# The last 256 rows of a gated cross-attention: the norm's weights multiplied in on GpSimd beside the squares, and one factor per row behind the root

## The chip, the cores and the metric

The kernel runs on one core of a Trainium2 chip. The metric is device time in microseconds (us) of one execution. The core has five engines that run their own queues of instructions and wait for each other through semaphores: TensorE (PE, matmuls; PEld its weight loads), VectorE (DVE), ScalarE (ACT), GpSimd (POOL) and SyncE (SP), which here issues nearly all transfers.

## The reference

Everything is float32. x has 8 batches of 1024 rows of 1024; the memory has 8 batches of 64 rows of 512. Cut to what is computed:

```
memory_proj = memory @ W_mem.T                          # 8 x 64 x 1024
scores      = x @ memory_proj.T / sqrt(1024)
attn        = softmax(scores)
context     = attn @ memory_proj                        # 8 x 1024 x 1024
gate        = sigmoid(concat(x, context) @ W_gate.T + b_gate)
fused       = x + gate * context
out         = fused * rsqrt(mean(fused**2) + 1e-6) * norm_w
```

The mean goes over the 1024 elements of a row. norm_w has one weight for each column.

## The kernel before

The kernel first projects the memory, and folds the context's part of the gate into a second projection of the memory, so that the only large product is x with the first half of W_gate. It works on 16 blocks (q = 0 to 15) of 512 rows each, a block being four tiles (t = 0 to 3) of 128 rows. The large product of a block uses a two-level scheme with fewer multiplications than the plain one: seven outer products, emitted in the order 1, 6, 7, 5, 4, 2, 3 (`ORDER`, L599), each of seven inner products (named A to F, A twice) in `outer_product` (L753). The inner sums of inputs (tiles `l`) and the sums `gate<-gate,u` run on GpSimd; the sums that read matmul results run on VectorE, all through the helper `tt` (L95). So L95 stands for many additions, and its rows are told apart by the names of their tiles.

The order of the work is written out by hand. Every inner product advances a counter `slot`; `at(slot, f, ...)` puts a function on a list that is emitted when the counter gets there (`step`, L646), and a loop at the end (L900) empties what is left. All instructions are kept in the order in which they are emitted on each engine, and each engine runs its queue in that order. The framework adds the waits between engines from the tiles that each instruction reads and writes.

In a block, outer products 5 and 4 complete the gate of tiles 2 and 3 (one half of 512 columns each), and 2 and 3 that of tiles 0 and 1: half 0 with outer product 2, half 1 with outer product 3. For each half, ScalarE takes the sigmoid (L657) and VectorE multiplies by the context, which lies in the accumulation buffer `pc` (L653). In blocks 0 to 14 x is added by a transfer, and the norm follows inside the next block's work.

The last block (q = 15) has functions of its own. x is loaded into a tile `xl` early (`load_last`, L702). `last_gated` (L709) multiplies by the context, adds x on VectorE (L714, in the profile `gate<-gate,xl`) and takes the sum of squares of the half on ScalarE (L719), the first half's sum being brought into a bias (L722). `sqrt_table` (L748) loads ScalarE's table for the root ahead of the squares of the last half. `last_root` (L727) takes the root per row, `last_norm` (L736) has VectorE take the reciprocal (L740, with half 0 alone), multiply a half by that number per row and by norm_w's columns in one instruction with two tensor inputs (L744), and has SyncE issue the store of the half (L98, 256 KB).

For tiles 3 and 2 this is placed among the inner products of the outer products 2 and 3 (L871, the case o == 4); so some L744 of tile 2 stand in VectorE's queue among the last sums. For tiles 1 and 0 (d = 1 goes ahead of c = 0) it comes after the last matmul. In VectorE's queue the end is: L744 of tile 2's second half, the sums with kE and kF, product with pc and addition of x for tile 1, the same for tile 0, then L740 and two L744 for tile 1, L740 and two L744 for tile 0. GpSimd's queue ends with three additions `gate<-gate,u` of outer product 3. ScalarE's ends with two sigmoids, the table load, and square and root of tile 1, then of tile 0.

Of the kernel before, what the change touches and what calls it, by code (L numbers as in the profile page):

```python
# [9 lines left out]
AF = mybir.ActivationFunctionType  # L10
ALU = mybir.AluOpType
# [4 lines left out]
P = 128  # L16
# [4 lines left out]
def tile_gated_cross_attention_rmsnorm(  # L21
# [42 lines left out]
    nc = tc.nc  # L64
# [4 lines left out]
    NQ = B * QPB  # L69
# [3 lines left out]
    H = 512  # L73
# [15 lines left out]
    pin = tc.keep_in_program_order  # L89
# [4 lines left out]
    def tt(eng, o, a, b, op):  # L94
        pin(eng.tensor_tensor(o, a, b, op))  # L95

    def load(o, i):
        pin(nc.sync.dma_start(o, i))  # L98

    def t4k(pool, shape, tag, name):  # L100
        return pool.tile(shape, F32, tag=tag, name=name)
# [33 lines left out]
    for k in range(KD):  # L135
        t = t4k(*((gpool, [P, D], "gate") if k < 7 else (apool, [P, D], "s4")), f"w2_{k}")
# [8 lines left out]
    nw_sb = const.tile([P, D], F32, name="nw_sb")  # L145
# [184 lines left out]
    A, S, L2, O = {}, {}, {}, {}  # L330
    sTs, attns, attnTs, scs, mps, mgs = {}, {}, {}, {}, {}, {}
    def where(q, t=0):
        return q // QPB, (q % QPB) * QT + t * P
# [258 lines left out]
    def at(slot, fn, *args):  # L592
        due.setdefault(slot, []).append(lambda: fn(*args))

    def mid(key, fn, *args):
        beside.setdefault(key, []).append(lambda: fn(*args))
# [47 lines left out]
    slot = 0  # L644
# [55 lines left out]
    xl, halves = {}, {}  # L700
# [35 lines left out]
    def last_norm(t, h):  # L736
# [8 lines left out]
        )  # L745
        load(out[b, n0 : n0 + P, cols], g)

    def sqrt_table():  # L748

        t = t4k(small, [P, 1], "warm", "warm")  # L750
        pin(nc.scalar.activation(t, eps_sb, AF.Sqrt))

    def outer_product(q, o, ext):  # L753
# [68 lines left out]
        if ext:  # L822
            row, h, g = ext
# [3 lines left out]
            for r, names in ((0, ("A", "F")), (1, ("E", "D"))):  # L827
                pc = ps_ctx.tile([P, H], F32, tag="ctx", name=f"pc{q}_{o}_{r}")
                for n in range(2):
                    cols = slice(h * H + n * C, h * H + (n + 1) * C)  # L830
# [36 lines left out]
        if o in (4, 3) and q + 1 == NQ:  # L867
            c, d = 2 * ext[0], 2 * ext[0] + 1
            if o == 3:
                sqrt_table()  # L870
            when = (4, 5, 7, 9, 11, 12) if o == 4 else (2, 4, 5, 6, 7, 8)  # L871
            at(slot + when[0], last_root, d)
            at(slot + when[1], last_root, c)
            for w_, (t, h_) in zip(when[2:], ((d, 0), (d, 1), (c, 0), (c, 1))):
                at(slot + w_, last_norm, t, h_)
        elif o in (4, 3):

            row = ext[0]
            c, d = 2 * row, 2 * row + 1
            for t in (d, c):  # L880
                at(slot + 5, residual, q, t)
            if row == 0:
                when = (17, 18, 23, 29, None, None)
            else:
                when = (17, 18, 23, 25, 29, 32)
            at(slot + when[0], square, q, c)
            at(slot + when[1], square, q, d)
            for w_, (t, h_) in zip(when[2:], ((c, 0), (c, 1), (d, 0), (d, 1))):
                if w_ is None:
                    mid((q + 1, 4), norm, q, t, h_)  # L890
                else:
                    at(slot + w_, norm, q, t, h_)
# [3 lines left out]
    for q in range(NQ):  # L896
        plan(q)
        for o, ext in ORDER:
            outer_product(q, o, ext)
    while due:  # L900
        slot = min(due)
# [27 lines left out]
```

## Time and profile before

| what | value |
|---|---|
| device time, median of 3 runs | 972.3 us (972.01 to 973.57) |
| the profiled execution's own time | 972.48 us |
| its span, first to last instruction | 970.7 us |
| busy: TensorE, VectorE, ScalarE, GpSimd | 958.1, 815.0, 329.2, 763.5 us |
| last matmul starts, length of the group of four | 959.69 us, 1.03 us |
| last GpSimd instruction | ends 959.49 us |
| second of the last two sigmoids ends | 961.91 us |
| table load for the root | 961.93 to 963.21 us |
| roots of tiles 1 and 0 end | 964.36 and 965.30 us |
| last four L744 | 964.59 to 966.01 and 966.12 to 967.54 us |
| last four stores issued | 965.37, 966.04, 966.90, 967.56 us |
| from issue to landing of such a store | 2.0 to 2.1 us |

Times inside the execution count from the start of the span. A row of the timeline has start, length, engine, line, operation, the tile written and the tiles read, the sizes and how many were merged; in brackets the idle time before it and who ended it. A row of a group has its count, busy time, mean length in ns and idle time ahead of it. "SPq" or "POOLq" is the engine's own queue of issuing and waiting instructions, which is not counted as busy.

### The profile page before, as it was taken

What the parts mean: (1) busy time and instruction counts of PE and PEld (TensorE: products, weight loads), DVE (VectorE), ACT (ScalarE), POOL (GpSimd) and SP (SyncE); (2) the same over time, 40 slices, a digit from 0 to 9 for tenths busy, and PEclk for the clock granted to TensorE, in tenths of its full rate; (3) what the DMA queues carried; (4) which work ended last, traced back from release to release, by engine and by line L of the source; (5) the groups of instructions that cost most, each with busy time, mean ns of one, the idle gap of its engine ahead of it and who ended that gap; (6) DMA issues with size and microseconds to landing.
All of it is one profiled execution on the core that took longest, in us unless ns stands there. A gap on an engine that the chain in (4) does not pass through costs nothing.

```text
span 970.7 us, 14400 instructions
## 1 busy us (share of the span) xinstructions
PE 958.1 (99%) x4986; PEld 773.3 (80%) x4986; DVE 815.0 (84%) x1483; ACT 329.2 (34%) x603; POOL 763.5 (79%) x889
## 2 busy tenths in 40 slices
PE   9999999999999999999999999999999999999995
PEld 8546878788888888788888888888888878888884
DVE  5988879879797988879797988979797978979787
ACT  2000234161423334162433324152333325152345
POOL 4998878778786968878786978878687878878692
PEclk9999999999999999999999999999999999999998
DMA  9957573472919374482918374381918465391712
GB/s 374 280 137 166 95 134 95 118 165 73 177 65 169 107 134 102 109 175 65 185 65 159 102 140 111 96 187 57 193 66 148 113 131 119 87 196 48 190 67 86
DMA packets 71159, 128.32 MB, mean 132 GB/s; under 512 B 12336, under 2 KB 49200, under 8 KB 70832
## 3 DMA queue, kind: packets, MB, share of 16 engines
q1 hardware_dynamic: 61760, 93.34, 36.7%
q0 software_dynamic: 9184, 33.56, 19.0%
q8 instruction: 39, 0.64, 0.3%
q10 hardware_dynamic: 144, 0.52, 0.2%
q14 instruction: 32, 0.26, 0.1%
HBM read 87.56 MB, written 41.68 MB: 133 GB/s over the span
## 4 chain that ended last, share of the span: by engine, by line
PE 97%; DVE 1%; DMA 1%; issue 0%; ACT 0%; DVEq 0%
PE kA L92 20%; PE pc L92 12%; PE kE L92 11%; PE kD L92 10%; PE kF L92 10%; PE kC L92 10%; PE kB L92 10%; PE psT L92 6%; PE pg L92 5%; PE pm L92 3%; DMA memq<-in_mem 1%; PE pa L438 0%; PE sc L412 0%; DVE gate L744 0%; DVE it L95 0%
## 5 line engine op out<-in xcount | busy, mean ns | idle before, releaser
L95 POOL TENSOR_TENSOR gate<-gate,u 128x256 f32<-128x256 f32 x336 | 287.5, 886 | 107.2 <-DVE u L95 107.2
L657 ACT ACTIVATE gate<-gate 128x512 f32<-128x512 f32 x128 | 80.6, 631 | 306.5 <-DVE gate L95 305.9
L95 POOL TENSOR_TENSOR l<-a 128x256 f32<-128x256 f32 x128 | 124.6, 974 | 21.6 <-PE kA L92 20.4
L344 DVE STREAM_TRANSPOSE a<-xq 128x512 f32<-128x512 f32 x128 | 137.9, 1099 | 2.9 <-DMA mgd<-mpq 2.9
L92 PE MATMUL pc<-mg,attnT 64*128 64x256 f32 x512 | 127.5, 389 | 0.0
L92 PE MATMUL kB<-it,l 128*128 128x256 f32 x448 | 115.1, 379 | 0.4 <-DVE gate L95 0.4
L92 PE MATMUL kD<-it,l 128*128 128x256 f32 x448 | 115.0, 379 | 0.0
L92 PEld LDWEIGHTS pc<-mg,attnT 64*128 64x128 f32 x512 | 90.6, 186 | 29.9 <-issue 21.2
L686 DVE SCALAR_TENSOR_TENSOR gate<-gate,ss,nw_sb 128x512 f32<-128x512 f32 x120 | 109.0, 918 | 1.1
L95 POOL TENSOR_TENSOR l<-s 128x256 f32<-128x256 f32 x96 | 79.3, 826 | 33.1 <-PE kF L92 30.3
L92 PE MATMUL kA<-w,a 128*128 128x256 f32 x384 | 98.6, 379 | 0.0
L92 PEld LDWEIGHTS kB<-it,l 128*128 128x128 f32 x448 | 85.0, 190 | 12.3 <-DVE gate L95 0.8
L92 PEld LDWEIGHTS kD<-it,l 128*128 128x128 f32 x448 | 85.1, 190 | 11.6
L95 DVE TENSOR_TENSOR gate<-gate,pc 128x512 f32<-128x512 f32 x128 | 86.8, 679 | 0.4 <-ACT gate L657 0.4
L95 DVE TENSOR_TENSOR gate<-gate,kE 128x256 f32<-128x256 f32 x112 | 45.5, 418 | 48.4 <-PE kE L92 42.3
L92 PEld LDWEIGHTS kA<-w,a 128*128 128x128 f32 x384 | 71.7, 190 | 9.5 <-DVE mg_c L95 0.2
L810 ACT COPY u<-kA 128x256 f32<-128x256 f32 x112 | 40.5, 361 | 110.5 <-PE kA L92 106.1
L92 PE MATMUL kE<-it,a 128*128 128x256 f32 x256 | 69.0, 392 | 0.0
L671 ACT ACTIVATE junk<-gate 128x1024 f32<-128x1024 f32 x60 | 63.5, 1059 | 11.2 <-DMA gate<-in_x 10.2
L95 DVE TENSOR_TENSOR u<-u,kB 128x256 f32<-128x256 f32 x112 | 45.7, 408 | 24.2 <-PE kB L92 21.6
L92 PE MATMUL kA<-t,s 128*128 128x256 f32 x256 | 65.8, 379 | 0.0
L92 PE MATMUL kF<-w,l 128*128 128x256 f32 x256 | 65.7, 379 | 0.0
(141 smaller groups left out, 2055.6 us busy)
## 6 DMA issues: line engine op xcount, KB each, us to landing
xq<-in_x SPq DMA_DIRECT2D x64, 512.0 KB, 10.1
gate<-in_x POOLq DMA_DIRECT2D x60, 512.0 KB, 8.1
out<-gate SPq DMA_DIRECT2D x60, 512.0 KB, 2.6
w<-in_w_gate_t SPq DMA_DIRECT2D x8, 512.0 KB, 11.0
w<-in_w_gate_t SPq DMA_DIRECT2D x2, 2048.0 KB, 16.2
mg<-mgd SPq DMA_DIRECT2D x16, 256.0 KB, 3.8
mpd<-mpT SPq DMA_DIRECT2D x4, 512.0 KB, 7.7
mgd<-mpq SPq DMA_DIRECT2D x16, 128.0 KB, 3.4
```

Source lines behind the costliest of these rows:

```text
L92: pin(nc.tensor.matmul(o, lhsT, rhs, start=start, stop=stop, skip_group_check=True))
L95: pin(eng.tensor_tensor(o, a, b, op))
L344: nc.vector.transpose(A[key][:, :, r * P : (r + 1) * P], chunks(xq[q][:, 4 * t : 4 * t + 4, :], KD)[:, half * KH : (half + 1) * KH],)
L657: pin(nc.scalar.activation(g, g, AF.Sigmoid))
L671: nc.scalar.activation(junk, O[q, t], AF.Square, accum_out=ss[:, t % 2 : t % 2 + 1])
L686: nc.vector.scalar_tensor_tensor(g[:, cols], g[:, cols], rstd[:, t % 2 : t % 2 + 1], nw_sb[:, cols], ALU.mult, ALU.mult,)
L810: pin(nc.scalar.copy(p1, kb["A"]))
```

## The change

For tiles 1 and 0 of the last block alone, the multiplication by norm_w is taken out of the instruction behind the root. GpSimd multiplies x + gate * context by norm_w into the tile `xl`, which is free once x has been added: both half-0 pieces behind its last additions, the half-1 pieces each behind the addition of x. ScalarE goes on squaring the unweighted sum. Behind the root, VectorE takes the reciprocal and multiplies a half by the number per row (`tensor_scalar`, no second tensor); of the last tile, half 0 is multiplied on ScalarE (a copy with a scale per row). The stores read `xl`: tile 1 half 0, tile 1 half 1, tile 0 half 1, and at the end tile 0 half 0. Tiles 2 and 3 go on as before.

```diff
+    def weigh(t, h):
+
+        cols = slice(h * H, (h + 1) * H)
+        tt(nc.gpsimd, xl[t][:, cols], O[NQ - 1, t][:, cols], nw_sb[:, cols], ALU.mult)
+
+    def last_scale(t, h, on_act):
+        b, n0 = where(NQ - 1, t)
+        rstd = halves[t][0][:, 2:3]
+        cols = slice(h * H, (h + 1) * H)
+        g = xl[t][:, cols]
+        if on_act:
+            pin(nc.scalar.activation(g, g, AF.Copy, scale=rstd))
+        else:
+            pin(nc.vector.tensor_scalar(g, g, rstd, None, ALU.mult))
+        load(out[b, n0 : n0 + P, cols], g)
+
+    def last_reciprocal(t):
+        rstd = halves[t][0][:, 2:3]
+        pin(nc.vector.reciprocal(rstd, rstd))
...
-            when = (4, 5, 7, 9, 11, 12) if o == 4 else (2, 4, 5, 6, 7, 8)
-            at(slot + when[0], last_root, d)
-            at(slot + when[1], last_root, c)
-            for w_, (t, h_) in zip(when[2:], ((d, 0), (d, 1), (c, 0), (c, 1))):
-                at(slot + w_, last_norm, t, h_)
+            if o == 4:
+                at(slot + 4, last_root, d)
+                at(slot + 5, last_root, c)
+                for w_, (t, h_) in zip((7, 9, 11, 12), ((d, 0), (d, 1), (c, 0), (c, 1))):
+                    at(slot + w_, last_norm, t, h_)
+            else:
+                for t in (d, c):
+                    at(slot, weigh, t, 0)
+                for i, t in enumerate((d, c)):
+                    at(slot + 2 + i, weigh, t, 1)
+                    at(slot + 2 + i, last_root, t)
+                at(slot + 4, last_reciprocal, d)
+                at(slot + 4, last_scale, d, 0, False)
+                at(slot + 4, last_scale, d, 1, False)
+                at(slot + 4, last_reciprocal, c)
+                at(slot + 4, last_scale, c, 1, False)
+                at(slot + 4, last_scale, c, 0, True)
```

## The prediction, on record before the run

> **What bounds the kernel now.** First the page: engine shares and the chain that ended last.
>
> ```profile
> PE 958.1 (99%) x4986; PEld 773.3 (80%) x4986; DVE 815.0 (84%) x1483; ACT 329.2 (34%) x603; POOL 763.5 (79%) x889
> ...
> PE 97%; DVE 1%; DMA 1%; issue 0%; ACT 0%; DVEq 0%
> ```
>
> TensorE is the bound until its last matmul. The order of instructions shows that the change leaves TensorE's queue as it was and touches only the ends of the other queues. So the whole question is the tail after 960.7 us. The chain in order of time (start, length, what) shows that tail:
>
> ```profile
> 959.86 0.88 PE kF L92 x4
> ...
> 961.28 0.63 ACT gate L657
> ...
> 961.93 1.28 ACT L751
> ...
> 963.42 0.62 ACT junk L719 x2
> ...
> 964.59 1.42 DVE gate L744 x2
> ...
> 966.12 0.75 DVE gate L744
> ```
>
> After TensorE come the second sigmoid, the table load of the root, squares, root, and four L744 normalizations on VectorE, each followed by its store. The stores:
>
> ```profile
> out<-gate SPq DMA_DIRECT2D x4, 256.0 KB, 2.1
> ```
>
> They are issued at 965.37, 966.04, 966.90 and 967.56. The last lands 2.06 us after its issue, at 969.62; barriers end the span at 970.70. In the view of DMA, bytes flow from 966.2 to about 969.2, and two transfers fill one unbroken stretch of 1.40 us: 0.70 each. So the tail has two limits: last issue + 2.06, and first issue + 0.85 (to the first bytes) + 4 x 0.70 + 0.40 (last bytes to landing) = first issue + 4.05, if the four come close together.
>
> Next the timeline, VectorE against GpSimd, for what happens when both read at once:
>
> ```profile
> 156.52 1.29 DVE L686 SCALAR_TENSOR_TENSOR gate<-gate,ss,nw_sb 128x512 f32<-128x512 f32 x1
> ...
> 156.54 0.72 POOL L95 TENSOR_TENSOR l<-s,l 128x256 f32<-128x256 f32 x1
> ...
> 375.92 0.74 DVE L686 SCALAR_TENSOR_TENSOR gate<-gate,ss,nw_sb 128x512 f32<-128x512 f32 x1
> ...
> 375.98 1.27 POOL L95 TENSOR_TENSOR l<-s,l 128x256 f32<-128x256 f32 x1
> ...
> 937.66 0.72 POOL L95 TENSOR_TENSOR l<-a 128x256 f32<-128x256 f32 x1
> ...
> 937.74 1.19 DVE L95 TENSOR_TENSOR gate<-gate,xl 128x512 f32<-128x512 f32 x1
> ...
> 958.15 0.75 DVE L744 SCALAR_TENSOR_TENSOR gate<-gate,halves,nw_sb 128x512 f32<-128x512 f32 x1
> ...
> 958.26 1.23 POOL L95 TENSOR_TENSOR gate<-gate,u 128x256 f32<-128x256 f32 x1
> ...
> 959.48 0.75 DVE L744 SCALAR_TENSOR_TENSOR gate<-gate,halves,nw_sb 128x512 f32<-128x512 f32 x1
> ```
>
> Of two such instructions one runs in its usual time (VectorE 0.69 to 0.75, GpSimd 0.73) and the other waits for it. GpSimd wins when it starts first, and even 0.02 us later (156.54); VectorE wins when it starts about 0.06 or more ahead (375.92). A waiting VectorE instruction ends 0.55 after GpSimd's (938.93 against 938.38); a waiting GpSimd instruction of 256 elements ends 0.59 after VectorE's (959.49 against 958.90).
>
> **What the Trainium skill says.** "SBUF — State Buffer", section "Who interferes with whom": VectorE with two SBUF inputs, or in a two-port mode such as `tensor_scalar` may enter, shares a read and write port pair with a GpSimd instruction that reads SBUF; whoever is first keeps it for the whole instruction and the other blocks. The rows above agree for two inputs; no `tensor_scalar` on SBUF stands in this trace. "VectorE: DVE Perf Modes", section "The perf-mode tier table": float32 `tensor_scalar` on SBUF reaches 2x. With the same page's (N+151)/0.96 ns, which gives 0.69 for 512 elements as the additions of x measure, 256 cycles are 0.42 us: an estimate. "ScalarE: Activation LUTs", section "What ACT_TABLE_LOAD costs": 186 ns + 0.833 ns per element, and 93 more for a pointer operand. The squares (0.61) agree; a scaled copy is then 0.70, an estimate.
>
> **The change, part by part.** Tile 1 goes ahead of tile 0; each has halves 0 and 1.
>
> Removed: four L744 of 0.75 on VectorE. Added: three scalings there at 0.42, one on ScalarE at 0.70, and four 128x512 multiplications on GpSimd. For these the set-up shows 1.27 with nothing in the way:
>
> ```profile
> L95 POOL TENSOR_TENSOR it<-w,it 128x512 f32<-128x512 f32 x4 | 5.1, 1274 | 0.2
> ```
>
> I take 1.27; multiplying instead of subtracting could cost nothing or some tenths more. Were all covered, the first scaling would end at 964.59 + 0.42 and its store be issued at 965.04 instead of 965.37. But the first two multiplications start while VectorE still has sums of the last half to do, and the other two start right behind an addition of x, so all four lie among VectorE's two-input instructions. Followed in order of time:
>
> 1. GpSimd's last addition ends at 958.26 + 1.23 = 959.49. The multiplication for (1,0) is queued behind it, its inputs ready, and starts about 0.04 before that end, 959.45 (GpSimd's instructions overlap so, 943.96 against 944.00), until 960.72. VectorE's L744 of tile 2 at 959.48 comes 0.03 too late, and ends at 960.72 + 0.55 = 961.27 instead of 960.23: **+1.04**. Queued behind it on VectorE: the additions of kE and kF, for which both sigmoids wait.
> 2. The multiplication for (0,0) waits for that L744 and ends at 961.27 + 0.59 + 0.54 (256 more elements: 1.27 - 0.73) = 962.40.
> 3. kE's addition ends at 961.61, kF's at 961.94; the second sigmoid ends at 962.81 (was 961.91); the table load follows, and squares can start at 964.23 (was 963.33).
> 4. Product with the context for tile 1: 962.30 to 962.98. Addition of x: to 963.70 (was 962.67). Product for tile 0: to 964.30.
> 5. The multiplication for (1,1), released by the addition of x, starts 0.08 later (956.44 after 956.36 shows that delay): 963.78 to 965.05. The addition of x for tile 0, due at 964.34, waits and ends at 965.60 (was 963.99): **+1.61**.
> 6. The root of tile 1 is ready at 965.26, but its reciprocal is behind that addition on VectorE: 965.52 to 965.68. The multiplication for (0,1) starts at 965.68 and ends at 966.95. The scaling of (1,0), due at 965.72, comes 0.04 too late; if it runs in the two-port mode it ends at 966.95 + 0.28 (its 256 cycles after the release) = 967.23; L744 there ended at 965.34: **+1.89**.
> 7. The rest: scaling (1,1) to 967.57, reciprocal of tile 0 to 967.65, scaling (0,1) to 968.10, ScalarE's (0,0) to 968.38. Stores are issued at 967.26, 967.62, 968.13 and 968.51. SyncE's issue takes 0.33, so it keeps up.
> 8. First issue + 4.05 = 971.31; last issue + 2.06 = 970.57 is covered by it. Against 969.62: **+1.7**.
>
> The store of (0,0) is last in SyncE's queue and waits for ScalarE; nothing is behind it. ScalarE's copy stands at the end of its queue, so it needs no table load that would stop others. GpSimd's closing DRAIN ends at 962.56, 3.07 after its last addition; after 966.95 that is 970.02, under the last landing.
>
> The profiled execution took 972.48 for a span of 970.70, 0.18 over the median of 972.3. 972.3 + 1.7 = **974.0**. The shorter instructions save 3.00 - 1.26 on VectorE and the waiting takes back more: slower by 0.17%, inside what counts as no change below.
>
> **The rivals.**
> - **The scaling doesn't take GpSimd's ports** (step 6 alone fails: 1x mode, 0.69). The first scaling ends at 966.41, its store is issued at 966.44, landing 970.49: +0.9, 973.2. For: no such row in the trace. Against: the skill's two pages.
> - **L744 of tile 2 is first in step 1.** The margin is 0.09. Then (1,0) ends at 961.36, (0,0) at 962.59, the first addition of x at 963.14, (1,1) at 964.49, the second addition at 965.04, (0,1) at 966.39, the first scaling at 966.67: issue 966.70, landing 970.75, +1.1: 973.4. Against: the row at 156.54.
> - **On the other side: no collision holds VectorE.** Mechanism: GpSimd's multiplications let VectorE's two-input instructions go first or run beside them, so the roots stay at 964.36 and 965.30. First issue 965.04, landing 969.09: -0.5, 971.8. It decides if each GpSimd multiplication ends before VectorE's next two-input instruction, under about 0.7 us at step 1. Against: all rows above, and 1.27 for the nearest multiplication.
> - **Slower by over 0.2%: GpSimd multiplies slower than it subtracts.** Three of its four instructions lie on the path (steps 1, 5, 6), so each 0.1 us of price costs 0.3. From 1.36 us on, the loss is over 1.94 us; at 1.5 it is 2.4, 974.7.
>
> **How the numbers follow.** About 0.2%, 1.94 us, is what a measurement can tell from no change here. Chances: both blocks as followed, 974.0, 0.52; scaling unblocked, 973.2, 0.17; L744 first, 973.4, 0.10; dearer multiplication, 974.3 to 974.9, 0.13; no collision, 971.8, 0.08. The main case spreads by some 0.3 with the transfers (0.70 to 0.76 each) and the run; about a fifth of it lies over 974.24. Slower by over 0.2%: 0.11 + 0.12 = 0.23. Faster by over 0.2% is under 970.36, beyond even the case without collisions: 0.02. Within: 0.75. The range 973.0 to 974.7 takes in 973.2, 973.4, the main case with its spread and half of the dearer one.
>
> **What would show it.** Step 1: L744 of tile 2 at 959.48 takes about 1.8 instead of 0.75, with GpSimd's first 128x512 ending 0.55 before it. Step 5: the last addition of x takes about 1.26 instead of 0.69. Step 6: the first scaling takes about 1.5 and the next 0.42; 0.69 for both would mean 1x. Step 8: one stretch of DMA of 2.8 us after 968. The prediction is wrong if a row of 128x512 on GpSimd isn't 1.27 when nothing holds it, or if the last store's landing isn't what ends the span.

## The result, and the profile after

| | before | changed |
|---|---|---|
| median of 22 runs each | 972.65 us | 974.32 us |
| ratio, 95% interval | | 1.0018 (1.0012 to 1.0024) |
| span of the profiled execution | 970.7 us | 972.5 us |
| last matmul's end to the end of the span (trace) | 9.98 us | 11.70 us |
| last four stores issued | 965.37, 966.04, 966.90, 967.56 | 967.34, 967.77, 968.40, 968.83 |

The kernel became slower by 0.18%. A ratio of 1 lies outside the interval, so the loss is real. The interval reaches past 0.2%, so the times don't settle on which side of the prediction's bound of 0.2% the loss lies. The prediction was 974.0 against 972.3, a ratio of 1.0017. Both kernels were measured some 0.3 us above these two figures, so it is the difference that is to be compared: 1.67 us here, 1.7 predicted. Nearly all of it lies behind the last matmul: the tail is 1.72 of the 1.81 us by which the two profiled spans differ. In its profile, the changed kernel is already 0.09 us late at the last group of four matmuls (it starts at 959.79 instead of 959.69); 0.09 is to be taken off its times below before they are set beside those of before.

The chain that ended last, in order of time, in the changed kernel (start, length, what):

```profile
960.88 0.40 issue
961.28 0.42 DVE gate L95
...
961.72 0.64 ACT gate L657
...
963.10 1.30 DVE gate L95 x2
...
964.43 1.26 DVE gate L95
...
965.87 1.84 DVE xl L761 x2
...
967.87 0.72 ACT xl L759
```

In the kernel before, the chain went from the second sigmoid over the table load and the squares to four L744. Here the table load and the squares are no longer in it. VectorE's own queue takes their place: the row at 963.10 is the first addition of x with the product behind it, the one at 964.43 the second addition, and then come the scalings at L761. The first row is 0.40 us in which VectorE's queue shows no wait: it is held by an L744 that is still under way. The timeline of both engines says why:

```profile
959.54 1.26 POOL L95 TENSOR_TENSOR xl<-gate,nw_sb 128x512 f32<-128x512 f32 x1
...
959.58 1.78 DVE L744 SCALAR_TENSOR_TENSOR gate<-gate,halves,nw_sb 128x512 f32<-128x512 f32 x1
...
960.77 1.71 POOL L95 TENSOR_TENSOR xl<-gate,nw_sb 128x512 f32<-128x512 f32 x1
...
963.87 1.27 POOL L95 TENSOR_TENSOR xl<-gate,nw_sb 128x512 f32<-128x512 f32 x1 [1.39 <-DVE gate L95]
...
964.43 1.26 DVE L95 TENSOR_TENSOR gate<-gate,xl 128x512 f32<-128x512 f32 x1
...
965.77 1.27 POOL L95 TENSOR_TENSOR xl<-gate,nw_sb 128x512 f32<-128x512 f32 x1 [0.62 <-DVE halves L766]
...
965.87 1.45 DVE L761 TENSOR_SCALAR xl<-xl,halves 128x512 f32<-128x512 f32 x1
...
967.24 0.47 DVE L761 TENSOR_SCALAR xl<-xl,halves 128x512 f32<-128x512 f32 x1
```

The second addition of x in the kernel before:

```profile
963.30 0.69 DVE L95 TENSOR_TENSOR gate<-gate,xl 128x512 f32<-128x512 f32 x1
```

Read the changed kernel's rows in pairs. GpSimd's first multiplication (1.26) starts 0.03 ahead of L744 of tile 2, which takes 1.78 instead of 0.75. That L744 holds GpSimd's second (1.71). The third holds the second addition of x (1.26 instead of 0.69), the fourth the first scaling (1.45). The next two scalings, with nothing beside them, take 0.47 and 0.49. None of the three VectorE instructions shows an idle time in brackets: they have started, and the waiting is inside their length. Nor is it the shared norm_w that holds them: the addition of x and the scaling don't read it.

The stores, from the view of DMA from 966 to 972.5 us (each digit is the busy share of the transfer engines in a slice of 0.16 us, in tenths):

```profile
DMA  0000000000000599999999999899993000000000
...
out<-xl SPq DMA_DIRECT2D x4, 256.0 KB, 2.4
```

The four now follow each other within 1.5 us (2.2 before), and their transfers fill one stretch of about 2.8 us without a gap, as the prediction's second limit has it (first issue + 4.05). The median from issue to landing is 2.4 us instead of 2.1; the last took 2.6 us.

### The profile page after: what moved, and what is told of

Its sections match the earlier page's. It is cut to its first block, busy times and chain, and to the rows that moved or that the text cites. A ratio compares the mean times of both kernels' runs of the same rounds, so it can differ in the third digit from the quotient of the medians.

```text
span 972.5 us, 14408 instructions
## 1 busy us (share of the span) xinstructions
PE 958.6 (99%) x4986; PEld 773.5 (80%) x4986; DVE 818.2 (84%) x1482; ACT 330.1 (34%) x604; POOL 767.9 (79%) x893
## 4 chain that ended last, share of the span: by engine, by line
PE 97%; DVE 1%; DMA 1%; issue 0%; ACT 0%; DVEq 0%; ACTq 0%
PE kA L92 20%; PE pc L92 12%; PE kE L92 11%; PE kD L92 10%; PE kF L92 10%; PE kC L92 10%; PE kB L92 10%; PE psT L92 6%; PE pg L92 5%; PE pm L92 3%; DVE gate L95 1%; DMA memq<-in_mem 1%; PE pa L438 0%; PE sc L412 0%; DVE it L95 0%
## 5 line engine op out<-in xcount | busy, mean ns | idle before, releaser
L92 PE MATMUL kC<-w,l 128*128 128x256 f32 x256 | 65.8, 379 | 0.1
```

The costliest lines, as they stand in the source:

```text
L92: pin(nc.tensor.matmul(o, lhsT, rhs, start=start, stop=stop, skip_group_check=True))
```

## The experiments

The theory, called port theory in the texts on record, is that a VectorE instruction with two tensors in SBUF, the memory on the core (or a scaling in its double-rate mode) and a GpSimd instruction that reads SBUF run one after the other. The rivals are that GpSimd's results come late and only their users wait, that GpSimd's work as such costs, and that the bunched stores cost. Each run below has its time against the kernel before, and the tail from the last matmul's end to the end of the span in its trace. A tile and its half are written as a pair: (1,0) is half 0 of tile 1.

| run | ratio to before (95%) | tail, us | against before's 9.98 |
|---|---|---|---|
| changed kernel | 1.0018 (1.0012 to 1.0024) | 11.70 | +1.72 |
| half 1 alone | 1.0010 (1.0003 to 1.0017) | 10.91 | +0.93 |
| half 0 alone | 1.0008 (1.0000 to 1.0016) | 10.65 | +0.67 |
| late start | 1.0011 (1.0005 to 1.0018) | 11.11 | +1.13 |
| three weighed | 1.0009 (1.0003 to 1.0016) | 10.76 | +0.78 |
| no weights | 0.9996 (0.9988 to 1.0004) | 9.55 | -0.43 |
| memsets | 0.9993 (0.9985 to 1.0001) | 9.61 | -0.37 |
| one weighed | 0.9999 (0.9991 to 1.0007) | 9.78 | -0.20 |
| GpSimd last | 1.0007 (0.9999 to 1.0015) | 10.82 | +0.84 |
| half 0, late start | 0.9998 (0.9990 to 1.0006) | 9.78 | -0.20 |

One us is 0.10%. The intervals are 0.6 to 0.8 us to either side, so differences of some tenths are read from the tails, and from single instructions, not from the times. Each tail comes from one profiled execution. How well two executions agree there is seen where the code is the same: in the kernel before and in the run with GpSimd last, the four stores are issued 4.65, 5.32, 6.18, 6.84 and 4.66, 5.32, 6.18, 6.84 us after the last matmul.

### Half 1 alone

```diff
-                for t in (d, c):
-                    at(slot, weigh, t, 0)
...
-                at(slot + 4, last_reciprocal, d)
-                at(slot + 4, last_scale, d, 0, False)
+                at(slot + 4, last_norm, d, 0)
                 at(slot + 4, last_scale, d, 1, False)
-                at(slot + 4, last_reciprocal, c)
-                at(slot + 4, last_scale, c, 1, False)
-                at(slot + 4, last_scale, c, 0, True)
+                at(slot + 4, last_norm, c, 0)
+                at(slot + 4, last_scale, c, 1, True)
```

> GpSimd multiplies only the half-1 pieces by the weights; half 0 is normalized by L744 as in the kernel before. Port theory (VectorE and GpSimd take turns when both read two tensors): L744 of tile 2 is back at 0.75 us, the first addition of x is at 0.69, the second waits for the multiplication of (1,1) and takes about 1.27, the first L744 of tile 1 waits for the multiplication of (0,1) and takes about 1.8; first store issued 1.1 later than before; time 0.95 us over before, 0.8 under the changed kernel. Rival (the results of GpSimd come late, and only instructions that use them wait): the second addition of x and the L744 of half 0 use none of them, so all keep 0.69 and 0.75, and the time is 0.2 under before.

Measured: L744 of tile 2 0.75, additions of x 0.69 and 1.26, tail +0.93. The first L744 of tile 1, from the timeline:

```profile
964.37 1.26 POOL L95 TENSOR_TENSOR xl<-gate,nw_sb 128x512 f32<-128x512 f32 x1 [0.63 <-DVE halves L740]
...
964.40 1.78 DVE L744 SCALAR_TENSOR_TENSOR gate<-gate,halves,nw_sb 128x512 f32<-128x512 f32 x1
```

That L744 reads tile 1's half 0 and GpSimd multiplies tile 0's half 1. Neither uses a result of the other, and yet L744 takes 1.78. So late results are not the cause.

### Half 0 alone

```diff
                     at(slot, weigh, t, 0)
                 for i, t in enumerate((d, c)):
-                    at(slot + 2 + i, weigh, t, 1)
                     at(slot + 2 + i, last_root, t)
...
-                at(slot + 4, last_scale, d, 1, False)
+                at(slot + 4, last_norm, d, 1)
                 at(slot + 4, last_reciprocal, c)
-                at(slot + 4, last_scale, c, 1, False)
+                at(slot + 4, last_norm, c, 1)
                 at(slot + 4, last_scale, c, 0, True)
```

> GpSimd multiplies only the half-0 pieces; half 1 is normalized by L744. Port theory: L744 of tile 2 takes 1.78 us as in the changed kernel, both additions of x take 0.69, the first scaling 0.47; first store issued about 0.65 later than before; the last landing is set by the third store, 0.6 us over before, 1.1 under the changed kernel. Rival (late results): L744 of tile 2 uses nothing of GpSimd's multiplications, so it keeps 0.75 and the time is about 0.2 under before.

Measured: L744 of tile 2 1.78, both additions of x 0.69, first scaling 0.49, tail +0.67. From its timeline:

```profile
959.74 1.78 DVE L744 SCALAR_TENSOR_TENSOR gate<-gate,halves,nw_sb 128x512 f32<-128x512 f32 x1
...
964.60 0.69 DVE L95 TENSOR_TENSOR gate<-gate,xl 128x512 f32<-128x512 f32 x1
...
965.79 0.49 DVE L761 TENSOR_SCALAR xl<-xl,halves 128x512 f32<-128x512 f32 x1
```

Step 1 of the prediction alone, with nothing of its steps 5 and 6, costs 0.67, what the shorter first scaling saves being taken off already. The last landing was that of the fourth store, issued 0.42 behind the third, and not the third's. The parts' losses add to 1.60 (0.93 + 0.67) and not to 1.72. They need not add, since each of the two runs has other instructions behind the root than the changed kernel; where the 0.12 come from was not followed up.

### Late start

```diff
+    def filler():
+        pin(nc.gpsimd.memset(t4k(small, [P, P], "fill", "fill"), 0.0))
...
+                at(slot, filler)
                 for t in (d, c):
                     at(slot, weigh, t, 0)
```

> The changed kernel with one small GpSimd memset (128x128, about 0.2 us, into a tile that nothing reads) ahead of its first multiplication, which so starts 0.15 or so behind L744 of tile 2 and not 0.03 ahead of it. Port theory with the tie rule of the prediction: L744 of tile 2 takes 0.75, the first multiplication of GpSimd 1.9; the first addition of x now waits (about 1.2), so does the second (about 1.2) and the first scaling (1.5). One added instruction makes the kernel faster: 0.55 us under the changed kernel, 1.15 over before. Rival (late results, or GpSimd's total work decides): 0.0 to 0.2 over the changed kernel.

Measured: tail +1.13, and 0.59 under the changed kernel's. From its timeline:

```profile
959.50 0.20 POOL L749 MEMSET fill<- 128x128 f32 x1
...
959.55 0.75 DVE L744 SCALAR_TENSOR_TENSOR gate<-gate,halves,nw_sb 128x512 f32<-128x512 f32 x1
...
959.67 1.76 POOL L95 TENSOR_TENSOR xl<-gate,nw_sb 128x512 f32<-128x512 f32 x1
...
962.05 1.15 DVE L95 TENSOR_TENSOR gate<-gate,xl 128x512 f32<-128x512 f32 x1
```

GpSimd's multiplication now comes 0.12 behind L744 and it is GpSimd that waits (1.76). The first addition of x waits in return (1.15), and the rest follows as in the changed kernel. Work was added and the tail got shorter. So not the amount of GpSimd's work decides, but when it starts.

### Three weighed

```diff
-                    at(slot + 2 + i, weigh, t, 1)
+                    if t == d:
+                        at(slot + 2 + i, weigh, t, 1)
...
-                at(slot + 4, last_scale, c, 1, False)
+                at(slot + 4, last_norm, c, 1)
```

> The changed kernel, but the last multiplication of GpSimd, for (0,1), is left to VectorE's L744 behind the root. Port theory: all is as in the changed kernel up to the second addition of x (1.26 us); the first scaling, with no GpSimd instruction beside it, takes 0.47 instead of 1.45 and the first store is issued 1.0 earlier; time 1.0 us under the changed kernel, 0.75 over before. Rival (the first scaling of 1.45 is what such an instruction costs, or it waits for its own data): it stays at 1.45, and the time is that of the changed kernel or above.

Measured: tail +0.78, 0.94 under the changed kernel's. The first two scalings, in one row of the timeline:

```profile
966.28 0.88 DVE L761 TENSOR_SCALAR xl<-xl,halves 128x512 f32<-128x512 f32 x2
```

Two take 0.88 here, overlapping; in the changed kernel they took 1.84. With GpSimd's fourth multiplication away, the scaling has its own 0.49. At 512 elements it is shorter than the 0.69 of an addition, which fits the double rate that the prediction took for it, and it was the multiplication for the other tile that held it.

### No weights

```diff
-                for t in (d, c):
-                    at(slot, weigh, t, 0)
...
-                    at(slot + 2 + i, weigh, t, 1)
...
-        g = xl[t][:, cols]
+        g = O[NQ - 1, t][:, cols]
```

> The changed kernel with GpSimd's four multiplications left out: the scalings read x + gate * context itself, so norm_w is not multiplied into tiles 1 and 0 of the last block. What the shorter instructions are worth with nothing in their way. Port theory: L744 of tile 2 0.75 us, both additions of x 0.69, scalings 0.48 each; first store issued 0.25 earlier than before, the four stores then follow each other without a gap and set the end: 0.4 us under before, 2.1 under the changed kernel. Store theory (the changed kernel is late because its four stores bunch, not because VectorE waits): they bunch here as well, and the time is over that of before.

Measured: tail -0.43, L744 0.75, additions of x 0.69, scalings 0.48 to 0.49, first store issued 0.26 earlier after the last matmul than before. From its timeline, and then its stores:

```profile
959.51 0.75 DVE L744 SCALAR_TENSOR_TENSOR gate<-gate,halves,nw_sb 128x512 f32<-128x512 f32 x1
...
963.33 0.69 DVE L95 TENSOR_TENSOR gate<-gate,xl 128x512 f32<-128x512 f32 x1
...
964.62 0.88 DVE L761 TENSOR_SCALAR gate<-gate,halves 128x512 f32<-128x512 f32 x2
```

```profile
out<-gate SPq DMA_DIRECT2D x4, 256.0 KB, 2.4
```

The four stores bunch here too, and the tail is still shorter than before. The last one takes 2.65 us to land, in the changed kernel 2.59, against 2.05 before. So the bunching lengthens both tails by half a microsecond or so, but it is not what sets them apart. This run is also the ceiling for this order of work: with the multiplications free, the change could have gained 0.43 us, 0.04%.

### Memsets in place of the multiplications

```diff
-        tt(nc.gpsimd, xl[t][:, cols], O[NQ - 1, t][:, cols], nw_sb[:, cols], ALU.mult)
+        pin(nc.gpsimd.memset(xl[t][:, cols], 1.0))
```

> The changed kernel with each of GpSimd's multiplications replaced by a memset of the same 128x512 piece of the same tile (estimate 0.5 us, from 0.196 for 128x128 and 0.098 for 128x1): the same writes, order and waits, but GpSimd reads nothing. x + gate * context and the weights are left out of the outputs of tiles 1 and 0 of the last block. Port theory in its narrow form (only GpSimd's reads hold up an instruction with two tensors): L744 of tile 2 0.75, additions of x 0.69, scalings 0.48; 0.4 us under before. Rival (any GpSimd instruction that touches memory at that time holds VectorE): L744 of tile 2 about 1.1, the second addition of x 0.7 to 0.9; 0.0 to 0.3 over before.

Measured: tail -0.37. The first of two memsets in a row, and L744 of tile 2 beside them:

```profile
959.86 0.52 POOL L751 MEMSET xl<- 128x512 f32 x1
...
959.90 0.75 DVE L744 SCALAR_TENSOR_TENSOR gate<-gate,halves,nw_sb 128x512 f32<-128x512 f32 x1
```

GpSimd starts 0.04 ahead and writes all through L744, which keeps its 0.75. So it is GpSimd's reading that holds an instruction with two tensors: writing alone, by the two memsets that together last from 959.86 to 960.83, did not. The scaling at 965.09 came after the last memset had ended (964.99), so whether a GpSimd instruction that only writes would hold a scaling stays open.

### One weighed

```diff
-                for t in (d, c):
-                    at(slot, weigh, t, 0)
-                for i, t in enumerate((d, c)):
-                    at(slot + 2 + i, weigh, t, 1)
-                    at(slot + 2 + i, last_root, t)
+                at(slot, filler)
+                at(slot, weigh, d, 0)
+                at(slot + 2, last_root, d)
+                at(slot + 3, last_root, c)
                 at(slot + 4, last_reciprocal, d)
                 at(slot + 4, last_scale, d, 0, False)
-                at(slot + 4, last_scale, d, 1, False)
-                at(slot + 4, last_reciprocal, c)
-                at(slot + 4, last_scale, c, 1, False)
-                at(slot + 4, last_scale, c, 0, True)
+                at(slot + 4, last_norm, d, 1)
+                at(slot + 4, last_norm, c, 0)
+                at(slot + 4, last_norm, c, 1)
```

> The part of the change that fits between VectorE's two-tensor instructions: the small memset, then GpSimd multiplies (1,0) alone; VectorE scales (1,0) and normalizes the three other halves by L744. Port theory: GpSimd waits for L744 of tile 2 (0.75) and ends 0.6 us ahead of the first addition of x (0.69), nothing on VectorE waits; the scaling takes 0.48, first store issued 0.25 earlier than before, last 0.2 earlier, the end 0.2 us under before: too little for the times, to be seen in the profile from TensorE's end. Rival (any GpSimd multiplication beside the tail costs VectorE): 0.3 or more over before.

Measured: tail -0.20; L744 of tile 2 0.75, both additions 0.69, the scaling 0.49. The multiplication, and what VectorE does beside it:

```profile
959.27 1.76 POOL L95 TENSOR_TENSOR xl<-gate,nw_sb 128x512 f32<-128x512 f32 x1
...
959.82 0.42 DVE L95 TENSOR_TENSOR gate<-gate,kE 128x256 f32<-128x256 f32 x1
960.50 0.42 DVE L95 TENSOR_TENSOR gate<-gate,kF 128x256 f32<-128x256 f32 x1 [0.27 <-PE kF L92]
960.93 0.69 DVE L95 TENSOR_TENSOR gate<-gate,pc 128x512 f32<-128x512 f32 x1
961.65 0.69 DVE L95 TENSOR_TENSOR gate<-gate,xl 128x512 f32<-128x512 f32 x1
```

GpSimd waits for L744 and is done at 961.03, 0.62 ahead of the addition of x. The sums with kE and kF and the product with pc read one input from matmul results, not from SBUF, and keep their length beside it (0.42, 0.42, 0.69). A GpSimd multiplication that lies there costs nothing. The gain is too small for the times: 0.9999.

### GpSimd last

```diff
+    def late_pool():
+        pin(nc.gpsimd.memset(halves[0][0][:, 2:3], 0.0))
...
+            if o == 3:
+                at(slot + 8, late_pool)
```

(In the kernel before.)

> The kernel before, with one GpSimd memset of 128x1 added behind VectorE's last L744 (it overwrites the root of tile 0 when that is no longer needed). Tests the cover of GpSimd's closing DRAIN, which ends 3.07 us after GpSimd's last instruction in the profiles of before and after. If that time is fixed, the memset ends at about 967.7 and the DRAIN at 970.8 on the clock of before, 0.8 us behind the last store's barrier: 0.8 us over before. Rival (the DRAIN waits for something else and is not tied to the last instruction): 0.0.

Measured: tail +0.84, with the stores issued at the same distances from the last matmul as before. The row of GpSimd's own queue at the closing line (shortest, median and longest in ns; first and last start):

```profile
L930 POOLq DRAIN  x3: 40/93/3187, 967.8 to 971.5; - x3
```

The long DRAIN starts at 967.81 and ends at 971.00, 3.07 after the memset's end at 967.93. In before (962.56 after 959.49) and in the changed kernel (970.11 after 967.04) it is 3.07 as well. It was covered there, as the prediction said. Here it ends the span.

### Half 0, late start

```diff
+                at(slot, filler)
                 for t in (d, c):
                     at(slot, weigh, t, 0)
```

(In the run with half 0 alone.)

> GpSimd multiplies only the half-0 pieces, as in the run with half 0 alone, but behind the small memset. Port theory: L744 of tile 2 takes 0.75 instead of 1.78; the first addition of x waits for the multiplication of (0,0) and takes about 1.15, which ScalarE's table load hides; the second addition takes 0.69; first scaling 0.48; stores issued 0.2 (first) to 0.5 (last) earlier than before; from the last matmul to the end of the span 9.6 us, against 9.98 before and 10.65 without the memset: 0.4 us under before, 1.0 under the run without the memset. Rival (GpSimd's work as such is what costs): as without the memset, 0.7 over before.

Measured: tail 9.78, -0.20, not the 9.6 expected; 0.87 under the same kernel without the memset. L744 0.74, and:

```profile
961.02 1.26 POOL L95 TENSOR_TENSOR xl<-gate,nw_sb 128x512 f32<-128x512 f32 x1
...
961.68 1.15 DVE L95 TENSOR_TENSOR gate<-gate,xl 128x512 f32<-128x512 f32 x1
```

The mechanism came as expected, the addition of x included (1.15), and it is hidden by the table load. The size was off: the stores were issued 0.2 to 0.4 earlier than before, but the last took 2.3 to land and not 2.06, which fits that the two ahead of it were still under way. Among the versions that leave nothing out, this one and the one with one piece weighed end ahead of the kernel before: both by 0.20 us in the profile, by nothing that the times show.

## Why the prediction was right

With 0.09 taken off the changed kernel's times, its steps stand so:

| step | end predicted | end measured |
|---|---|---|
| 1: L744 of tile 2 | 961.27 | 961.27 |
| 2: multiplication (0,0) | 962.40 | 962.39 |
| 3: second sigmoid | 962.81 | 962.78 |
| 4: first addition of x | 963.70 | 963.71 |
| 5: second addition of x | 965.60 | 965.60 |
| 6: multiplication (0,1) | 966.95 | 966.95 |
| 6: first scaling | 967.23 | 967.23 |
| 7: first store issued | 967.26 | 967.25 |
| 7: last store issued | 968.51 | 968.74 |
| 8: last landing | 971.31 | 971.33 |

- Step 1 was the bold one: which of two instructions 0.03 us apart would go first. It was read from two near-ties of the profile before, and late start shows the other outcome, with the price that the rival gave it (+1.1 predicted, +1.13 in the tail). It did not hang on the edge of the rule (see below the list), since GpSimd was ahead: by 0.03 in the prediction, and by 0.03 in the profile.
- Steps 5 and 6 hold, shown by taking their multiplications away: half 0 alone, without both, has the second addition back at 0.69; three weighed, without the last, has the scaling back at 0.49.
- Step 7 has terms that were mis-sized. A scaling takes 0.47 to 0.49, not 0.42, and starts 0.11 behind the reciprocal's end, not 0.04. In the run without weights, where no scaling reads what GpSimd wrote, it starts 0.03 behind; with memsets in place of the multiplications it is 0.11 again. So the other 0.07 come with reading a tile that GpSimd wrote, even one that it finished long before. The third store was issued 0.18 late for this, and the last, which followed it by 0.43 and not 0.38, 0.23 late. It cost nothing: the last store alone (its issue + 2.06) would have landed at 970.80, and the limit from the first issue (+ 4.05; measured 4.07) ended the span, as the prediction had it.
- The removal (3.00 - 1.26 us of VectorE's work) was counted right as worth little: without any multiplication the tail gains 0.43, where the rival without collisions said 0.5.
- The rival of a dearer multiplication falls: 1.26 and 1.27 with nothing in the way, as the subtraction's 1.27. The rival of a scaling that doesn't take GpSimd's ports falls with the 1.45 against 0.49.
- The Trainium skill says on the page "SBUF — State Buffer", section "Who interferes with whom", that the one that issues first keeps the shared ports and the other blocks, and that a GpSimd instruction that only writes doesn't hold an instruction with two tensors. The runs agree with both: 1.78 and 1.71 us in one order, 0.75 and 1.76 in the other, and 0.75 beside the memsets.

The prediction's rule that VectorE wins from about 0.06 us ahead isn't sharp at its edge. Elsewhere in the profile before, VectorE is 0.06 ahead and waits all the same:

```profile
760.10 1.33 DVE L686 SCALAR_TENSOR_TENSOR gate<-gate,ss,nw_sb 128x512 f32<-128x512 f32 x1
...
760.16 0.72 POOL L95 TENSOR_TENSOR l<-s,l 128x256 f32<-128x256 f32 x1
```

Where the expected gain went: an instruction that VectorE could do in 0.75 was split into 1.27 on GpSimd and 0.48 on VectorE. GpSimd was idle there, but the way to memory that it needs was not. Three of the four multiplications were given back as 1.03, 0.57 and 0.97 us of waiting inside VectorE instructions. Of these 2.57 us, 2.15 reach the end (tail 11.70 against 9.55 without the multiplications). What the shorter instructions save pays for 0.43 of them, and 1.72 are left.

## What to carry to other kernels

Before moving elementwise work to an idle engine, look at what the busy engine does in those very microseconds: two engines that share a way to memory take turns while both read through it. In this kernel that was so for instructions of VectorE with two inputs in SBUF, and for the scaling. Look at instructions that are longer than their group's usual length, not at idle times, since such a wait is not shown as one. At the end of a kernel, work out which limit the stores set before making the last instruction shorter.

## What was not expected of the hardware

GpSimd's closing DRAIN ends 3.07 us after its last instruction in every profile here, even when that is a memset of 128x1 that takes 0.10 us. Placed last, such an instruction can set the end of a kernel alone (+0.84 us). And a memset of 0.20 us on an idle engine shortened the tail by 0.59 and by 0.87 us, in two kernels, by deciding who goes first.
